# SyncE fetches 102 token columns in place of 96 and ScalarE 62 in place of 52, with other pacing tables

## The chip, the cores and the metric

One core of a Trainium2 chip runs the whole kernel; the other cores are idle. The metric is the device time of one execution in microseconds (us), lower being better. The time before is the median of three runs.

## What is computed

The reference looks up rows of embedding tables for 16384 samples, averages them, joins them and passes them through a small network. The part that matters here is the first lookup: 32 token rows of 300 floats (1200 bytes) per sample, out of a table of 50000 rows, averaged over the 32.

```python
tok = word_emb[token_idx].mean(axis=1)      # (16384, 32) indices, rows of 300 floats
e1 = emb_mh1[mh1_idx].mean(axis=1)          # 20 indices per sample; e2, e3 likewise
o1 = emb_oh1[oh1_idx]                       # 1 index per sample; o2, o3, o4 likewise
emb = concatenate([tok, e1, e2, e3, o1, o2, o3, o4], axis=1)
wide = ...                                  # sums of one more column of the same small tables
h = relu(emb @ W1 + b1); h = relu(h @ W2 + b2); h = relu(h @ W3 + b3)   # 748 -> 1024 -> 512 -> 256
y = sigmoid(h @ Wd + bd + wide)
```

## The kernel before

**Tiles and steps.** The batch is cut into 128 tiles of 128 samples. One Python loop (`for step in range(n_steps)`) writes out the program of all engines: a tile has 11 steps, and 27 more steps (`WAKE`) let the last tiles finish, 1435 in all. Each engine runs its own instructions in the order in which this loop wrote them, and waits on semaphores where one needs another's result.

**What a step does.** VectorE compares indices with a counter and writes one-hot rows (`hot`, the group `hot<-own,sc`). ScalarE scales a half of them (`hot<-hot`), which is the "one-hot scaling" of the change. TensorE multiplies one-hots into counts (`pc<-hot`), ScalarE copies the counts out (`cnt<-pc`), TensorE multiplies counts with the small tables (`pg<-terms,cnt`), and VectorE sums that into the features (`g<-pg`). Beside this TensorE runs the network's layers (`ph<-x,w_sb`, `ph<-odd,w_sb`, `ph<-even,w_sb`), whose results ScalarE copies out (`odd<-ph`, `even<-ph`).

**Token rows.** For one sample tile and one of the 32 token positions, 128 rows have to be fetched. The text calls this a *column*. There are 128 x 32 = 4096 columns, and three ways to fetch one:

- GpSimd (POOL) issues one indirect DMA for the whole column (`gather`, L260, `tok_rows<-in_word_emb_dram,it`). Two columns make a group, 16 groups a tile; there are six buffers of one group each (`TOK_BUFS`), and a group is added three groups after it was asked for (`TOK_LAG`).
- SyncE (SP) issues 128 plain DMAs of one row each (`row`, L244, `fetched<-in_word_emb_dram`). It first reads the 128 row addresses into registers, 32 at a time (`load`, L275, a `TENSOR_LOAD`), so a column is four times one load and 32 rows. The indices themselves come by one DMA per column (`load_column`, L233, `columns<-in_idx_dram`), and VectorE turns them into byte offsets (`column_offsets`, `columns<-columns`). SP may fetch token position 31 of a tile, and has two buffers (`FETCH_BUFS`).
- ScalarE (ACT) does the same for token position 30 (`fetched_scalar<-in_word_emb_dram`), with 16 addresses per load. Its rows stand in its queue before and after the one-hot scaling of each step (`scalar_rows(step, SCALAR_BEFORE)`, then `one_hots`, then `scalar_rows(step, SCALAR_AFTER)`).

VectorE adds each column to the tile's sum in PSUM (`own<-own,tok_rows`, `own<-own,fetched`), and the last add of a tile writes the features (`g<-own,...`). These adds stand in one queue with the one-hots of the following steps.

**Who fetches what** is settled when the program is written, by `RowFetches`. It lays fetches of a fixed length (`steps`) end to end, and gives each one the next tile that is not needed before that fetch ends plus `FETCH_MARGIN`, three steps. A column that neither SP nor ACT takes goes to POOL. `wanted_at(t)` is the step in which tile t's sum is due: `16 / 1.4196 = 11.27` steps from tile to tile. Before, `FETCH_STEPS` is 14.5 steps for a column on SP: the first starts at step 31.16 and serves tile 5, the last starts at step 1408.66 and serves tile 127, 96 columns in all. ACT puts out five rows a step (25.6 steps a column), 52 columns. POOL keeps 4096 - 96 - 52 = 3948.

`prepare` has the column's indices loaded four steps ahead of the start of its fetch, and the offsets computed one step ahead (`COLUMN_AHEAD`, `COLUMN_LAG`). SP's queue also holds the index loads of each pair of tiles (`it`, `ix`) and the stores of results (`out_dram<-x`), all L233.

Of the kernel before, what the change touches and what calls it, by code (L numbers as in the profile page):

```python
# [22 lines left out]
N_TOK, TOK_D = 32, 300  # L23
# [5 lines left out]
TOK_BUFS = 6  # L29
HOT_BUFS = 2  # L30
FETCH_FROM = 4
FETCH_STEPS = 14.5
FETCH_MARGIN = 3.0
FETCH_BUFS = 2
COLUMN_AHEAD = 4
# [1 line left out]
LOADS = 32  # L37
LANES = 8
ROW_SEMAPHORES = 8
SCALAR_FROM = 8  # L40
SCALAR_BEFORE, SCALAR_AFTER = 3, 2
SCALAR_RATE = SCALAR_BEFORE + SCALAR_AFTER
SCALAR_MARGIN = 5.0
SCALAR_LOADS = 16
# [332 lines left out]
def kernel(  # L377
# [679 lines left out]
    tiles = B // P  # L1057
# [13 lines left out]
    def summed_at(t):  # L1071

        n = n_groups * (t + 1) + TOK_LAG
        return n / FRONT_PACE if n < front else FRONT_STEPS + (n - front) / pace
# [2 lines left out]

        return summed_at(t) - 1.0

    by_sync = RowFetches(N_TOK - 1, False, summed_at(FETCH_FROM) - FETCH_STEPS - FETCH_MARGIN, FETCH_STEPS, tiles, LOADS)  # L1080
    scalar_steps = P / SCALAR_RATE
    by_scalar = RowFetches(
        N_TOK - 2, True, int(summed_at(SCALAR_FROM) - scalar_steps - SCALAR_MARGIN), scalar_steps, tiles - 2, SCALAR_LOADS
    )
    sync_rows = Paced_rows(by_sync, FETCH_STEPS)

# [162 lines left out]
```

## Time and profile before

| | |
|---|---|
| time before, median of 3 runs | 4987.18 us (4986.96 to 4992.43) |
| profiled execution: time, span | 4988.4 us, 4986.6 us |
| granted TensorE clock, mean | 0.991 |
| busy: TensorE, VectorE, ScalarE, GpSimd | 4794.8, 3642.8, 2728.2, 3739.3 us |
| token columns by POOL, SP, ACT | 3948, 96, 52 |
| rows issued one by one by SP, ACT | 12288, 6656 |

The span runs from the first to the last instruction. In the lines below, PE is TensorE, PEld its weight loads, DVE VectorE, ACT ScalarE, POOL GpSimd, SP SyncE. A "q" behind a name (SPq, ACTq) is the engine's sequencer, which issues DMAs and loads registers; this is not counted as busy, so SP has no busy time at all. "x3948" counts instructions. In a group, "busy, mean ns of one" is followed by the idle time of the engine just ahead of these instructions and what ended it; "issue" means that nothing in the profile ended it. TensorE's busy time is modelled and includes pipelined waiting.

### The profile page before, as it was taken

What the parts mean: (1) busy time and instruction counts of PE and PEld (TensorE: products, weight loads), DVE (VectorE), ACT (ScalarE), POOL (GpSimd) and SP (SyncE); (2) the same over time, 40 slices, a digit from 0 to 9 for tenths busy, and PEclk for the clock granted to TensorE, in tenths of its full rate; (3) what the DMA queues carried; (4) which work ended last, traced back from release to release, by engine and by line L of the source; (5) the groups of instructions that cost most, each with busy time, mean ns of one, the idle gap of its engine ahead of it and who ended that gap; (6) DMA issues with size and microseconds to landing.
All of it is one profiled execution on the core that took longest, in us unless ns stands there. A gap on an engine that the chain in (4) does not pass through costs nothing.

```text
span 4986.6 us, 110478 instructions
## 1 busy us (share of the span) xinstructions
PE 4794.8 (96%) x36356; PEld 3712.3 (74%) x36356; DVE 3642.8 (73%) x6908; ACT 2728.2 (55%) x3658; POOL 3739.3 (75%) x3955
## 2 busy tenths in 40 slices
PE   6699999999999999999999999999999999999999
PEld 4577777777777777777777777767767888888898
DVE  5777777777777777777777777777777777777763
ACT  5455555555555555555555555555555555555552
POOL 7777777777777777777777777777777777777765
PEclk9899999999999999999999999999999999999999
DMA  7444444444444444444444444444444444444443
GB/s 204 127 130 130 130 131 129 131 130 130 131 131 131 130 130 130 131 131 130 130 131 130 131 131 130 130 131 129 131 130 130 130 131 130 131 131 130 131 120 95
DMA packets 305354, 653.28 MB, mean 131 GB/s; under 512 B 157083, under 2 KB 176667, under 8 KB 304775
## 3 DMA queue, kind: packets, MB, share of 16 engines
q0 software_dynamic: 189504, 606.67, 44.7%
q1 hardware_dynamic: 94471, 31.50, 2.9%
q10 hardware_dynamic: 20800, 8.04, 0.8%
q8 instruction: 284, 4.65, 0.4%
q14 instruction: 295, 2.42, 0.2%
HBM read 645.67 MB, written 0.07 MB: 129 GB/s over the span
## 4 chain that ended last, share of the span: by engine, by line
PE 46%; POOL 16%; DMA 15%; DVE 12%; issue 8%; ACT 1%; ACTq 1%; SPq 1%; DVEq 0%; POOLq 0%
PE ph L113 24%; PE pg L113 16%; POOL tok_rows L260 16%; DMA tok_rows<-in_word_emb_dram,it 15%; PE pc L113 6%; DVE own L113 5%; DVE hot L113 4%; DVE g L113 1%; ACTq L244 1%; SPq L244 1%; ACTq L275 0%; ACT cnt L113 0%; DVE x L113 0%; DVE columns L113 0%; ACT hot L113 0%
## 5 line engine op out<-in xcount | busy, mean ns | idle before, releaser
L260 POOL DMA_INDIRECT tok_rows<-in_word_emb_dram,it x3948 | 3738.4, 947 | 1215.6 <-issue 931.5
L113 DVE TENSOR_TENSOR own<-own,tok_rows 128x300 f32<-128x300 f32 x3601 | 1714.5, 476 | 822.0 <-DMA tok_rows<-in_word_emb_dram,it 746.8
L113 ACT ACTIVATE hot<-hot 64x768 bf16<-64x768 bf16 (+1 forms) x1408 | 1155.3, 821 | 1698.2 <-DVE hot L113 1514.8
L113 PE MATMUL pg<-terms,cnt 128*128 128x195 bf16 x17664 | 1721.6, 249 | 31.0 <-DVE g L113 30.7
L113 PEld LDWEIGHTS pg<-terms,cnt 128*128 128x128 fp8e3 x17664 | 1523.8, 98 | 83.7 <-DVE g L113 39.1
L113 PE MATMUL ph<-x,w_sb 128*128 128x384 f32 (+5 forms) x4932 | 1472.1, 436 | 16.5 <-ACT odd L113 11.3
L113 DVE TENSOR_TENSOR hot<-own,sc 128x1656 bf16<-128x1656 bf16 (+1 forms) x1408 | 1386.6, 985 | 86.0 <-PE pc L113 80.4
L113 ACT ACTIVATE cnt<-pc 128x828 uint16<-128x828 f32 (+1 forms) x1408 | 1186.3, 843 | 257.0 <-PE pc L113 170.8
L113 PEld LDWEIGHTS ph<-x,w_sb 128*128 128x128 f32 (+1 forms) x4932 | 829.8, 191 | 306.5 <-ACT odd L113 20.9
L113 PE MATMUL ph<-odd,w_sb 128*128 128x384 f32 (+2 forms) x3328 | 983.2, 434 | 7.7 <-ACT odd L113 7.3
L113 PEld LDWEIGHTS pc<-hot 128*128 128x128 bf16 x8192 | 589.5, 98 | 494.8 <-issue 217.6
L113 PE MATMUL pc<-hot 128*128 128x138 bf16 x8192 | 733.2, 225 | 92.0 <-ACT hot L113 58.7
L113 PEld LDWEIGHTS ph<-odd,w_sb 128*128 128x128 f32 x3328 | 558.7, 191 | 204.7 <-ACT odd L113 15.8
L113 DVE TENSOR_REDUCE g<-pg 128x130 f32<-128x390 f32 (+1 forms) x512 | 259.7, 507 | 216.0 <-PE pg L113 213.1
L113 ACT ACTIVATE odd<-ph,b_sb 128x384 f32<-128x384 f32 (+2 forms) x515 | 270.0, 524 | 134.4 <-PE ph L113 68.8
L113 PE MATMUL ph<-even,w_sb 128*128 128x384 f32 (+2 forms) x832 | 250.0, 436 | 3.3 <-ACT even L113 2.9
L113 PEld LDWEIGHTS ph<-even,w_sb 128*128 128x128 f32 x832 | 142.3, 191 | 56.8 <-ACT even L113 4.1
L113 DVE TENSOR_TENSOR x<-pc,scale 128x768 f32<-128x768 f32 x127 | 120.9, 952 | 74.8 <-PE pc L113 74.0
L113 ACT ACTIVATE even<-ph,b_sb 128x384 f32<-128x384 f32 (+2 forms) x208 | 108.7, 523 | 88.4 <-PE ph L113 65.8
L113 PE MATMUL pc<-ident,g 128*128 128x128 f32 x762 | 106.5, 276 | 11.7 <-ACT cnt L113 7.5
L113 PEld LDWEIGHTS pc<-ident,g 128*128 128x128 f32 x762 | 82.9, 142 | 15.8 <-ACT cnt L113 11.7
L113 DVE COPY sc<-pc 128x512 bf16<-128x512 bf16 x64 | 44.0, 687 | 55.1 <-PE pc L113 55.0
(54 smaller groups left out, 673.0 us busy)
## 6 DMA issues: line engine op xcount, KB each, us to landing
fetched<-in_word_emb_dram SPq DMA_DIRECT2D x12288, 1.2 KB
fetched_scalar<-in_word_emb_dram ACTq DMA_DIRECT2D x6656, 1.2 KB
tok_rows<-in_word_emb_dram,it POOLq DMA_INDIRECT x3948
ix<-in_idx_dram SPq DMA_DIRECT2D x64, 64.0 KB
w_sb<-in_W_dram SPq DMA_DIRECT2D x6, 512.0 KB
it<-in_idx_dram SPq DMA_DIRECT2D x64, 32.0 KB
w_sb<-in_W_dram SPq DMA_DIRECT2D x1, 2048.0 KB
odd<-in_mh_dram SPq DMA_DIRECT2D x3, 682.5 KB
```

The costliest lines, as they stand in the source:

```text
L113: lambda: call(*args, **operands), self.name, self.name, aps + list(named.values()), outs
L244: return queue.add_instruction(mybir.InstDMACopy(name=self.nc.get_next_instruction_name(), engine=queue.engine, mode="Copy", ins=whole(sou ...
L260: return self.nc.gpsimd.indirect_dma_start(out=out, out_offset=None, in_=table, in_offset=bass.IndirectOffsetOnAxis(ap=index, axis=0),)
```

## The change

```diff
-FETCH_STEPS = 14.5
+FETCH_STEPS = 13.5
...
-SCALAR_BEFORE, SCALAR_AFTER = 3, 2
+SCALAR_BEFORE, SCALAR_AFTER = 4, 2
 SCALAR_RATE = SCALAR_BEFORE + SCALAR_AFTER
...
-    by_sync = RowFetches(N_TOK - 1, False, summed_at(FETCH_FROM) - FETCH_STEPS - FETCH_MARGIN, FETCH_STEPS, tiles, LOADS)
+    by_sync = RowFetches(N_TOK - 1, False, summed_at(FETCH_FROM) - FETCH_STEPS - FETCH_MARGIN, FETCH_STEPS, tiles - 1, LOADS)
```

A column on SP is given 13.5 steps in place of 14.5. The planner then places 102 columns: the first starts at step 32.16 and serves tile 5 as before; the last two start at steps 1382.16 and 1395.66 and serve tiles 124 and 126. Tile 127 is no longer open to SP (`tiles - 1`). ACT puts out six rows a step, so a column has 21.33 steps, and it gets 62 columns. POOL keeps 4096 - 102 - 62 = 3932. TensorE's instructions and their order stay the same.

ScalarE's queue about a sixth into the program, where `hot_76` and `hot_77` are the two one-hot buffers, `cnt` the counts and L244 a token row, before:

```order
1216 L113 ACTIVATE hot_76<-hot_76 64x6x128
1217 L244 DMA fetched_scalar_83<-in_word_emb_dram 1x1200 x2
1218 L113 ACTIVATE cnt_78<-pc_95 128x138x6
1219 L244 DMA fetched_scalar_83<-in_word_emb_dram 1x1200 x3
1220 L113 ACTIVATE hot_77<-hot_77 64x6x128
1221 L275 TENSOR_LOAD columns
1222 L244 DMA fetched_scalar_82<-in_word_emb_dram 1x1200 x2
```

and after:

```order
1217 L113 ACTIVATE cnt_78<-pc_95 128x138x6
1218 L244 DMA fetched_scalar_83<-in_word_emb_dram 1x1200 x4
1219 L113 ACTIVATE hot_77<-hot_77 64x6x128
1220 L275 TENSOR_LOAD columns
1221 L244 DMA fetched_scalar_83<-in_word_emb_dram 1x1200 x2
1222 L113 ACTIVATE cnt_78<-pc_94 128x138x6
```

One more row stands between a copy of the counts and the next one-hot scaling.

VectorE's queue at the end of tile 9's token sum, where `tok_rows` are columns of POOL, `fetched_80` a column of SP, and `hot` the one-hots of the next steps, before:

```order
382 L113 TENSOR_TENSOR hot_77<-own,sc_74 128x1656
383 L113 TENSOR_TENSOR own<-own,tok_rows_64 128x300
384 L113 TENSOR_TENSOR g_84<-own,tok_rows_64 128x300
385 L113 COPY sc_75<-pc_94 128x2x128x2
386 L113 TENSOR_TENSOR hot_76<-own,sc_74 128x1656
```

and after:

```order
382 L113 TENSOR_TENSOR hot_77<-own,sc_74 128x1656
383 L113 TENSOR_TENSOR own<-own,fetched_80 128x300
384 L113 TENSOR_TENSOR g_84<-own,tok_rows_64 128x300
385 L113 COPY sc_75<-pc_94 128x2x128x2
386 L113 TENSOR_TENSOR hot_76<-own,sc_74 128x1656
```

Tile 9 is one of the tiles whose last column comes from SP now and came from POOL before; the one-hots of the next step stand behind its add.

SP's queue at the end of the program, where `fetched_80` and `fetched_81` are its two buffers and `out_dram` the stores of results, before:

```order
1266 L244 DMA fetched_81<-in_word_emb_dram 1x1200 x32
1267 L275 TENSOR_LOAD columns
1268 L244 DMA fetched_81<-in_word_emb_dram 1x1200 x13
1269 L233 DMA out_dram<-x 1x128
1270 L244 DMA fetched_81<-in_word_emb_dram 1x1200 x19
1271 L233 DMA out_dram<-x 1x128 x3
```

and after:

```order
1326 L244 DMA fetched_81<-in_word_emb_dram 1x1200 x13
1327 L275 TENSOR_LOAD columns
1328 L244 DMA fetched_81<-in_word_emb_dram 1x1200 x32
1329 L275 TENSOR_LOAD columns
1330 L244 DMA fetched_81<-in_word_emb_dram 1x1200 x32
1331 L233 DMA out_dram<-x 1x128 x5
```

The last row of SP's last column has moved ahead of two more stores, since that column serves tile 126 in place of 127.

## Prediction

> **What bounds the kernel now.** I began with the page: the costliest groups and the list of DMA issues.
>
> ```profile
> PE 4794.8 (96%) x36356; PEld 3712.3 (74%) x36356; DVE 3642.8 (73%) x6908; ACT 2728.2 (55%) x3658; POOL 3739.3 (75%) x3955
> L260 POOL DMA_INDIRECT tok_rows<-in_word_emb_dram,it x3948 | 3738.4, 947 | 1215.6 <-issue 931.5
> L113 DVE TENSOR_TENSOR own<-own,tok_rows 128x300 f32<-128x300 f32 x3601 | 1714.5, 476 | 822.0 <-DMA tok_rows<-in_word_emb_dram,it 746.8
> ...
> fetched<-in_word_emb_dram SPq DMA_DIRECT2D x12288, 1.2 KB
> fetched_scalar<-in_word_emb_dram ACTq DMA_DIRECT2D x6656, 1.2 KB
> ```
>
> TensorE looks fullest, but its busy time is modelled. POOL shows 75%, yet its idle time is mostly "issue", that is, nothing held it. The timeline of POOL and the stretches say what that means:
>
> ```profile
> 2009.62 0.94 POOL L260 DMA_INDIRECT tok_rows<-in_word_emb_dram,it  x1 [0.30 <-issue]
> 2010.87 0.94 POOL L260 DMA_INDIRECT tok_rows<-in_word_emb_dram,it  x1 [0.30 <-issue]
> ...
> 500.00:1000.00 500.00, 491.04 (x3608) 361.25 (x3606) 372.84 (x708) 278.30 (x361) 378.02 (x401) 0.99 0.49 130
> 4000.00:4500.00 500.00, 495.17 (x4055) 439.25 (x4054) 375.33 (x707) 286.20 (x396) 377.99 (x401) 1.00 0.49 131
> ```
>
> A gather starts every 1.25 us (0.94 and 0.30 of issue), and early as well as late 401 of them fill 500 us (the fifth engine column): 401 x 1.25 = 501. POOL has no gap, and VectorE waits 746.8 us for its columns. POOL sets the pace, and TensorE is close behind.
>
> The page shows no busy time for SP at all, so I asked for its queue: the timeline of SP, then its register loads over the whole span and in three stretches (first and last start stand behind the durations).
>
> ```profile
> 2013.42 5.69 SPq L244 DMA_DIRECT2D fetched<-in_word_emb_dram  x18
> 2019.15 0.56 SPq L233 DMA_DIRECT2D columns<-in_idx_dram  x1
> 2019.76 45.20 SPq L244 DMA_DIRECT2D fetched<-in_word_emb_dram  x123
> ...
> L275 SPq TENSOR_LOAD <-columns x384: 2025/2127/2391, 142.9 to 4905.2; - x192
> L275 SPq TENSOR_LOAD <-columns x25: 2042/2127/2178, 1835.7 to 2129.9; - x25
> L275 SPq TENSOR_LOAD <-columns x28: 2026/2127/2192, 844.4 to 1176.4; - x28
> L275 SPq TENSOR_LOAD <-columns x41: 2030/2128/2289, 4218.2 to 4713.9; - x41
> ...
> L113 DVE TENSOR_SCALAR columns<-columns x296: 203/218/477, 142.4 to 4870.7; 1x128 int32<-1x128 int32 x148
> ```
>
> Four loads make a column. Over the span a column comes every 4 x (4905.2 - 142.9) / 383 = 49.74 us; in the three stretches every 49.03 (24 intervals), 49.19 (27) and 49.57 (40). The plan gives it 14.5 steps. A step lasts (4870.7 - 142.4) / 1377 = 3.434 us, since the offsets of SP's first and last column are computed in steps 30 and 1407. So the plan's 14.5 steps are 49.8 us, and SP uses nearly all of them: it is the second engine at its limit, and the page hides it.
>
> **The change, part by part.**
>
> *POOL loses 16 gathers*: 16 x 1.25 = 20 us less. This is all the gain there is: a span of 4967, if nothing else binds.
>
> *SP gets 13.5 steps a column*: 13.5 x 3.434 = 46.4 us, and 46.2 with POOL's relief. What does SP need? From below, built up from rows: the stretch of 123 rows above holds four loads, so a row takes (45.20 - 4 x 2.127) / 123 = 0.298 us. The rest of its queue is in this view of L233:
>
> ```profile
> L233 SPq DMA_DIRECT2D columns<-in_idx_dram x96: 534/554/606, 100.7 to 4852.5; - x96
> L233 SPq DMA_DIRECT2D it<-in_idx_dram x64: 402/414/3305, 1.0 to 4709.5; - x64
> L233 SPq DMA_DIRECT2D ix<-in_idx_dram x64: 589/612/1623, 1.5 to 4709.9; - x64
> L233 SPq DMA_DIRECT2D out_dram<-x x52: 217/785/835, 316.2 to 4981.2; - x52
> ```
>
> 128 x 0.298 + 4 x 2.127 + 0.55 = 47.2; it, ix and out add 64 x (0.414 + 0.612) + 52 x 0.785 = 106 us, 1.1 a column: 48.3 us. From above: 49.6, the slowest stretch. I take 48.9: the fastest stretch (49.03), as nothing there can be less than SP's work by much, less 0.1 because the 106 us are spread over 102 columns. SP is then short of 2.5 us in each column and falls behind the plan for good. The slack of a single column (3 to 14 steps between its planned end and its tile's due step) is used up within about ten columns. From there on VectorE stands at `own<-own,fetched`, the next one-hots stand behind it in its queue, and ScalarE, TensorE and (when the six buffers are full) POOL behind these. The kernel becomes as slow as SP's queue.
>
> How long is that queue? The first column's load starts one step later than before, 142.9 + 3.4 = 146.3. The tile of the last column but one (124) is due 4.5 steps after its planned end, so this one is late and the last is not: tile 126 is due 27 steps after that column's start, and the last column needs 14.2. So 101 columns count: 146.3 + 101 x 48.9 = 5085. What follows tile 124's sum was in the trace of before:
>
> ```profile
> 4846.28 0.47 DVE L113 TENSOR_TENSOR g<-own,fetched_scalar 128x300 f32<-128x300 f32 x1
> 4881.91 29.36 SPq L244 DMA_DIRECT2D fetched<-in_word_emb_dram  x79
> ...
> 4954.79 0.95 POOL L260 DMA_INDIRECT tok_rows<-in_word_emb_dram,it  x1 [0.31 <-DVE own L113]
> 4959.97 0.47 DVE L113 TENSOR_TENSOR g<-own,tok_rows 128x300 f32<-128x300 f32 x1
> ```
>
> From 4846.3 to the end of the span, 4986.6, are 140 us, with as many gathers as after, but for one. I add 3 us for the landing of the last rows (an estimate; a gather took 3.49 us in the chain). POOL can then be three groups ahead, six gathers or 7.5 us, but TensorE is at 96% and can hardly follow, so I take nothing off. The sum is 5085 + 3 + 140 = 5228 of span. Against the span before that is +241: 102 columns short of 2.5 us, less some 14 of slack. The profiled execution took 4988.4, 1.2 above the median, and its span 0.6 below it; so 5229 on the median's scale.
>
> *ScalarE* issues 10 columns more: 1280 rows and 80 loads. What stands around them, in its timeline and the waits:
>
> ```profile
> 1998.37 3.49 DMA tok_rows<-in_word_emb_dram,it
> 2006.96 0.81 ACTq L244 DMA_DIRECT2D fetched_scalar<-in_word_emb_dram  x3
> 2007.82 0.84 ACT L113 ACTIVATE hot<-hot 64x768 bf16<-64x768 bf16 x1 [0.29 <-DVE hot L113]
> ...
> L275 ACTq TENSOR_LOAD <-columns x416: 1178/1294/1532, 255.1 to 4816.2; - x139
> ACT hot L113 <- DVE hot L113: 1514.8, 947, 5.7
> DVE own L113 <- DMA fetched<-in_word_emb_dram: 11.2, 3, 6.7
> ```
>
> (The first line is the chain's gather, used above.) A row is 0.27 us, 3 in 0.81. The queue grows by 1280 x 0.27 + 80 x 1.29 = 449 us over the run. In 947 of 1408 steps ScalarE came early to the scaling and waited for VectorE, 1.6 us on average, so the fourth row lies in that wait. In the other 461 it can lengthen the step by up to 0.27, 124 us in all at most; but each step has 2.5 / 13.5 = 0.19 us to spare once SP sets the pace, which covers most of it. I cost it at 0 and keep 0 to 40 for the range. If SP did not bind, this cover would be gone.
>
> *The rest*: VectorE computes offsets for 16 more columns, two instructions each of 0.22, 7 us spread over a VectorE that is idle a quarter of the time: nothing. Its adds are as many as before. Rows of SP and ACT may get in each other's way a little more; the 0.298 holds that as it was, and I leave it to the range.
>
> **The rivals.**
>
> *SP keeps up, and the gain comes through.* For that a row would have to take (46.4 - 8.5 - 0.55 - 1.1) / 128 = 0.283 us, or waits must hide in the 49. Against it: no stretch shows less than 49.03 a column. Then 4967, faster by 0.4%; the point of decision is 46.4 us a column. The Trainium skill's "DMA: Bandwidth & Descriptors", section "Issuing engines are not separate DMA queues", says that starting DMAs from several engines only saves the issue time on the sequencer, and that this is usually small next to the DMA itself. By it SP would have room, and this rival would hold. The trace does not agree here: 128 issues at 0.298 us fill SP's sequencer.
>
> *SP is slower than 46.4, but less so: part of the 49 is waiting.* What speaks for it is the view of SP's waits:
>
> ```profile
> SPq L275 <- DVE own L113: 220.3, 73, 43.4
> SPq L275 <- DVE hot L113: 27.7, 13, 3.8
> SPq L275 <- DVE g L113: 13.6, 4, 6.5
> ```
>
> Without the first wait (43.4, ahead of the first column) that is 218 us. If all of it were real, a column would need 49.74 - 218 / 96 = 47.5, and the span would be 146 + 101 x 47.5 + 143 = 5086. But the view finds a release up to the end of an instruction, and each of these loads lasts 2.13 us by itself, 90 x 2.13 = 192: most of the 218 is the loads.
>
> *ScalarE becomes a second brake.* If each step lengthened by 0.27 on top of SP's pace (the row ahead of the scaling, with PE waiting behind it), 461 to 1408 steps would add 124 to 380 us: some 5350 to 5600. The waits above speak against it.
>
> *No change*: SP would need just about 46.5 us. Nothing points there.
>
> **How the numbers follow.** SP-bound at 48.3 to 49.6 a column: 0.85, span 5167 to 5299 by 101 x -0.6 and 101 x 0.7. SP part waiting: 0.06, near 5086. ScalarE a second brake: 0.04. SP keeps up: 0.03. No change: 0.02. The range of 5175 to 5285 leaves out the other cases and the outer edges of the first, where the build-up (48.3) and the slowest stretch (49.6, with late waits) are least likely. Within 0.2% (10 us) counts as no change.
>
> **What would show it.** In the changed kernel's trace: SP's loads at an even 48.9 us a column up to about 5130, in place of 49.74 with waits; POOL's idle time ended by `DVE own`, with fewer than 401 gathers in 500 us (about 380); a wait of `DVE own` for `fetched` of 200 us or more in all, where there were three of 11.2 us in all; the chain of waits running through SP's rows; ScalarE's waits for `hot` longer, not shorter. I am wrong if SP's loads come every 46.4 us, or if POOL still starts a gather every 1.25 us throughout.

## The result and the profile after

The changed kernel takes 5280.68 us (median of 4 runs, 5274.67 to 5283.33), the kernel before 4987.07 on the same chip: a ratio of 1.0585 [1.0566, 1.0603], 5.9% slower. The forecast was 5229 with a range of 5175 to 5285. The profiled execution took 5282.48 us, its span 5280.7.

The page of the changed kernel: busy time, the chain of waits by engine and by line, the costliest group, and the list of DMA issues.

```profile
PE 4875.9 (92%) x36356; PEld 3763.6 (71%) x36356; DVE 3643.8 (69%) x6940; ACT 2732.5 (52%) x3658; POOL 3726.0 (71%) x3939
PE 41%; SPq 32%; DVE 8%; issue 7%; DMA 5%; POOL 2%; ACT 2%; ACTq 2%; DVEq 0%
SPq L244 25%; PE ph L113 22%; PE pg L113 14%; SPq L275 6%; PE pc L113 5%; DVE hot L113 3%; DVE own L113 3%; DMA columns<-in_idx_dram 3%; POOL tok_rows L260 2%; DMA tok_rows<-in_word_emb_dram,it 2%; ACTq L244 1%; ACT hot L113 1%; SPq L233 1%; DVE g L113 1%; ACT cnt L113 1%
L260 POOL DMA_INDIRECT tok_rows<-in_word_emb_dram,it x3932 | 3725.1, 947 | 1520.5 <-issue 905.4
...
fetched<-in_word_emb_dram SPq DMA_DIRECT2D x13056, 1.2 KB
fetched_scalar<-in_word_emb_dram ACTq DMA_DIRECT2D x7936, 1.2 KB
```

Every engine does what it did before, in nearly as much busy time (TensorE 1.7% more), and has lost share: no engine with busy time has become the bound. POOL's group costs 13 us less, and its idle time is 305 us more (1215.6 before). What has entered the chain is SP: its queue holds 32% of it, the 128-row columns (L244) first and their register loads (L275) second. Before, it held 1%, and POOL 16%:

```profile
PE 46%; POOL 16%; DMA 15%; DVE 12%; issue 8%; ACT 1%; ACTq 1%; SPq 1%; DVEq 0%; POOLq 0%
```

SP's register loads over the span (count, duration ns min/median/max, first and last start), and two stretches of 500 us (busy time and count of PE, PEld, DVE, ACT and POOL, granted clock, DMA share, GB/s):

```profile
L275 SPq TENSOR_LOAD <-columns x408: 2026/2127/2372, 145.0 to 5149.4; - x136
500.00:1000.00 500.00, 466.82 (x3324) 341.49 (x3322) 351.28 (x669) 260.97 (x339) 352.64 (x373) 0.97 0.46 122
2500.00:3000.00 500.00, 472.53 (x3381) 346.37 (x3380) 353.84 (x675) 263.04 (x342) 357.28 (x379) 0.98 0.47 124
```

A column of SP comes every 4 x (5149.4 - 145.0) / 407 = 49.18 us. The plan wanted 13.5 steps of 3.434 us, 46.4. SP got faster by 0.56 us a column (49.74 before), and no more. POOL gets 373 to 379 gathers into 500 us, where 401 went before.

Where the lateness arrives is in the view of waits (us in total, times, longest), the first two lines of before, the others of the changed kernel:

```profile
DVE own L113 <- DMA tok_rows<-in_word_emb_dram,it: 769.8, 757, 4.3
POOL tok_rows L260 <- DVE own L113: 166.0, 510, 3.3
...
POOL tok_rows L260 <- DVE own L113: 436.4, 650, 13.3
ACT hot L113 <- DVE own L113: 340.9, 262, 3.2
DVE columns L113 <- DMA columns<-in_idx_dram: 291.9, 71, 8.5
DVE own L113 <- DMA fetched<-in_word_emb_dram: 182.6, 20, 15.1
DVE own L113 <- DMA tok_rows<-in_word_emb_dram,it: 121.2, 105, 5.1
```

VectorE used to wait for POOL's columns, 769.8 us in all. It now waits 121.2 for those, and 474.5 us for what comes out of SP's queue: the rows themselves (182.6) and, which the forecast did not foresee, the indices of the column four steps ahead (291.9), whose load stands in the same queue between SP's rows. POOL then waits for VectorE: 436.4 us, 166.0 before.

One such hold in the timelines of VectorE, SP and POOL:

```profile
4957.60 1.01 DVE L113 TENSOR_TENSOR hot<-own,sc 128x1656 bf16<-128x1656 bf16 x1
4972.35 0.48 DVE L113 TENSOR_TENSOR own<-own,fetched 128x300 f32<-128x300 f32 x1 [13.73 <-DMA fetched<-in_word_emb_dram]
4972.86 0.47 DVE L113 TENSOR_TENSOR g<-own,fetched_scalar 128x300 f32<-128x300 f32 x1
...
L275 SPq TENSOR_LOAD <-columns x1: 2114/2114/2114, 4966.5 to 4966.5; - x1
...
4961.24 0.95 POOL L260 DMA_INDIRECT tok_rows<-in_word_emb_dram,it  x1 [0.30 <-issue]
4974.91 0.94 POOL L260 DMA_INDIRECT tok_rows<-in_word_emb_dram,it  x1 [12.73 <-DVE own L113]
```

VectorE stands 13.73 us at the add of a column of SP (tile 120). POOL puts out one more gather at 4961.24 with 0.30 us of issue before it, then its buffers are full and it stands 12.73 us, until VectorE has gone on. It looks like the chain of the forecast: SP late, VectorE at its add, POOL behind. Which of SP's rows the add waits for is another matter; the section on the prediction comes back to it. The 13.73 us are the time of four steps.

### The profile page after: what moved, and what is told of

Its sections match the earlier page's. It is cut to its first block, busy times and chain, and to the rows that moved or that the text cites. A ratio compares the mean times of both kernels' runs of the same rounds, so it can differ in the third digit from the quotient of the medians.

```text
span 5280.7 us, 112655 instructions
## 1 busy us (share of the span) xinstructions
PE 4875.9 (92%) x36356; PEld 3763.6 (71%) x36356; DVE 3643.8 (69%) x6940; ACT 2732.5 (52%) x3658; POOL 3726.0 (71%) x3939
## 4 chain that ended last, share of the span: by engine, by line
PE 41%; SPq 32%; DVE 8%; issue 7%; DMA 5%; POOL 2%; ACT 2%; ACTq 2%; DVEq 0%
SPq L244 25%; PE ph L113 22%; PE pg L113 14%; SPq L275 6%; PE pc L113 5%; DVE hot L113 3%; DVE own L113 3%; DMA columns<-in_idx_dram 3%; POOL tok_rows L260 2%; DMA tok_rows<-in_word_emb_dram,it 2%; ACTq L244 1%; ACT hot L113 1%; SPq L233 1%; DVE g L113 1%; ACT cnt L113 1%
## 5 line engine op out<-in xcount | busy, mean ns | idle before, releaser
L113 PE MATMUL pg<-terms,cnt 128*128 128x195 bf16 x17664 | 1751.6, 251 | 38.1 <-DVE g L113 38.0
L113 PEld LDWEIGHTS pg<-terms,cnt 128*128 128x128 fp8e3 x17664 | 1549.8, 99 | 93.0 <-DVE g L113 42.5
L113 PE MATMUL ph<-x,w_sb 128*128 128x384 f32 (+5 forms) x4932 | 1495.2, 441 | 28.0 <-ACT odd L113 23.5
L113 PEld LDWEIGHTS ph<-x,w_sb 128*128 128x128 f32 (+1 forms) x4932 | 842.1, 193 | 325.2 <-ACT odd L113 30.2
L113 PE MATMUL ph<-odd,w_sb 128*128 128x384 f32 (+2 forms) x3328 | 998.6, 439 | 13.6 <-ACT odd L113 13.1
L113 DVE TENSOR_SCALAR columns<-columns 1x128 int32<-1x128 int32 x328 | 80.5, 246 | 299.6 <-DMA columns<-in_idx_dram 291.9
L113 DVE TENSOR_TENSOR own<-own,fetched 128x300 f32<-128x300 f32 x102 | 48.2, 472 | 183.4 <-DMA fetched<-in_word_emb_dram 182.6
```

Of the source, the lines that this page charges most:

```text
L113: lambda: call(*args, **operands), self.name, self.name, aps + list(named.values()), outs
```

## The experiments

Theory A is the forecast's: SP needs about 49 us a column, the plan gives 46.4, and SP's queue sets the end. Against it stood: ScalarE's fourth row is the brake; the wait for the indices is a loss of its own; the threshold is all or nothing. Each ratio is against the kernel before on the same chip; an edit is shown against the changed kernel unless the text says otherwise.

**Each half of the change alone.** First only ScalarE's half:

```diff
-FETCH_STEPS = 13.5
+FETCH_STEPS = 14.5
...
-by_sync = RowFetches(..., tiles - 1, LOADS)
+by_sync = RowFetches(..., tiles, LOADS)
```

> ScalarE's part alone: six rows a step, 62 columns on ScalarE, SP back at 96 columns and 14.5 steps; POOL keeps 3938 gathers. Theory A (SP's queue sets the end of the changed kernel): SP again has 49.8 us for a column that needs about 49.2, so POOL sets the pace and the ten gathers fewer come through: 10 x 1.25 = 12.5 us, 4975 us (4968 to 4983). Rival B (the fourth row ahead of the one-hot scaling lengthens the steps): slower than before, 5030 us or more.

Then only SP's half:

```diff
-SCALAR_BEFORE, SCALAR_AFTER = 4, 2
+SCALAR_BEFORE, SCALAR_AFTER = 3, 2
```

> SP's part alone: 102 columns at 13.5 steps, ScalarE back at three and two rows and 52 columns. Theory A: SP's loads come every 49.2 us a column as in the changed kernel, and the time is the same, 5281 us (5265 to 5290). Rival B: with the fourth row gone the time falls by what that row cost, to 5200 us or less.

ScalarE's half alone: 4981.86 us, ratio 0.9990 [0.9981, 1.0000]. SP's half alone: 5278.90 us, ratio 1.0585 [1.0567, 1.0602], the whole loss. SP's loads and the waits, of ScalarE's half and then of SP's:

```profile
L275 SPq TENSOR_LOAD <-columns x384: 2025/2127/2362, 143.0 to 4903.2; - x192
DVE own L113 <- DMA fetched<-in_word_emb_dram: 11.7, 3, 6.3
```

```profile
L275 SPq TENSOR_LOAD <-columns x408: 2027/2126/2378, 145.0 to 5151.5; - x136
DVE columns L113 <- DMA columns<-in_idx_dram: 304.6, 69, 9.2
DVE own L113 <- DMA fetched<-in_word_emb_dram: 191.3, 20, 15.1
```

With 52 columns on ScalarE SP still comes every 4 x (5151.5 - 145.0) / 407 = 49.2 us, so ScalarE's extra rows neither slow SP's queue nor the step. That rival is out. ScalarE's half gained 5 us of the 12.5 that ten gathers cost (10 x 1.25). Part of the difference shows late in the program, in two stretches of 200 us of ScalarE's half:

```profile
4000.00:4200.00 200.00, 197.69 (x1603) 174.64 (x1601) 145.74 (x275) 111.57 (x156) 149.25 (x158) 1.00 0.48 129
4600.00:4800.00 200.00, 193.75 (x1736) 177.45 (x1736) 144.03 (x272) 112.17 (x167) 147.60 (x156) 1.00 0.48 128
```

POOL puts out 158 and 156 gathers where 160 fit (161 and 158 before), and TensorE is busy 97 to 99%, as before: the gathers taken from POOL no longer make it faster there, and TensorE is probably the next limit. This reading was not tested by itself.

**Indices earlier.** Is the index wait (291.9 us) a loss of its own, or only where SP's lateness shows first?

```diff
-COLUMN_AHEAD = 4
+COLUMN_AHEAD = 8
```

> The changed kernel with the indices of a column asked for eight steps ahead of its fetch in place of four. VectorE's new wait for these indices (columns from in_idx, 292 us in the changed kernel's trace) should fall under 60 us. Theory A: that wait is only the form in which SP's lateness reaches VectorE; it comes back as a wait for the fetched rows, SP's pace stays at 49.2 us a column, and the time at 5265 to 5285 us. Rival C (the wait for indices, not the number of rows in SP's queue, is what costs): 5281 - 200 or more, under 5100 us.

5274.29 us, ratio 1.0574 [1.0557, 1.0592], 6 us better than the change. The waits and SP's loads:

```profile
DVE columns L113 <- DMA columns<-in_idx_dram: 29.7, 11, 6.2
DVE own L113 <- DMA fetched<-in_word_emb_dram: 381.7, 27, 28.6
L275 SPq TENSOR_LOAD <-columns x408: 2023/2127/2397, 144.7 to 5141.0; - x136
```

262 us of one wait went, and 199 us came in another. SP's column stays at 4 x (5141.0 - 144.7) / 407 = 49.1. A wait that is removed while the queue behind it stays too long is only moved.

**Half a step back.** If SP's need is about 49.2 us, 14.0 steps (48.1 us) should be short by 1.1 us a column and not by 2.8.

```diff
-FETCH_STEPS = 13.5
+FETCH_STEPS = 14.0
```

> The changed kernel with 14.0 steps a column on SP in place of 13.5: 99 columns. Theory A: 14.0 steps are 48.0 us, short of 49.2 by 1.2 us a column; SP's queue ends about 150 us earlier, and the time is about 5105 us (5080 to 5125), still slower than before. Rival D (slower only because the plan is pressed past a threshold of slack, in all or nothing): 4970 or 5280 us.

5093.88 us, ratio 1.0213 [1.0196, 1.0230], with 99 columns on SP.

```profile
L275 SPq TENSOR_LOAD <-columns x396: 2023/2128/2384, 142.9 to 5001.3; - x198
DVE columns L113 <- DMA columns<-in_idx_dram: 162.7, 49, 7.2
DVE own L113 <- DMA fetched<-in_word_emb_dram: 106.1, 11, 14.0
```

Again 4 x (5001.3 - 142.9) / 395 = 49.2 us a column, whatever the plan says; the loss follows the shortfall times the columns and is not all or nothing. As a rough sum, with the plan's slack and POOL's relief left aside, 98 x 1.1 = 108 us, measured 107; with 13.5 steps 101 x 2.8 = 283, measured 294.

**A dearer queue under the old plan.** The sharpest test leaves all columns where they were before and makes only SP's queue dearer: eight loads of 16 addresses in place of four of 32 (against the kernel before).

```diff
-LOADS = 32
+LOADS = 16
```

> The kernel of e7_loads16 a third time: the kernel before with SP reading its addresses 16 at a time, eight loads a column in place of four; the same 96 columns and 3948 gathers. Where the kernel before takes its 4987 us, theory A: a column on SP grows from 49.0 to about 50.7 us, over its 49.8, and the kernel takes 5050 us (5030 to 5080), with VectorE waiting for SP's rows; rival B (only the moved columns or ScalarE matter): 4987 us. Where the kernel before takes over 7000 us, a step lasts about 4.9 us and SP's column has 71 us: no difference over 0.3%.

5053.61 us against 4987.70, ratio 1.0134 [1.0117, 1.0151]. POOL has all its 3948 gathers, ScalarE all its rows.

```profile
L275 SPq TENSOR_LOAD <-columns x768: 1135/1232/1492, 142.9 to 4977.7; - x192
DVE columns L113 <- DMA columns<-in_idx_dram: 202.3, 58, 7.7
DVE own L113 <- DMA fetched<-in_word_emb_dram: 36.6, 9, 12.3
POOL tok_rows L260 <- DVE own L113: 260.8, 637, 9.5
```

Eight loads of 1.232 us are 1.35 us more than four of 2.127. A column comes every 8 x (4977.7 - 142.9) / 767 = 50.43 us where the plan gives 49.8, and the same waits appear as in the changed kernel, smaller. So SP's queue sets the time in both, and with 32 addresses a load the kernel before stood just under that line.

**Two kernels on a chip where this program is slower.** The same test was first made on another chip, twice, and with it the opposite one: the changed kernel with a cheaper queue, 112 rows of a column singly and the last 16 partitions by one DMA of table rows 0 to 15. That kernel leaves out the fetch of those 16 rows.

```diff
+if not by_scalar and p >= P - 16:
+    if p == P - 1:
+        rest = dict(out=tile_rows[P - 16 : P, :], in_=word[0:16, :])
+        program.record(lambda: queue.dma_start(**rest), "SP", lane, [], [rest["out"]], batch=batch)
...
```

> The kernel before with SP reading its addresses 16 at a time in place of 32: eight loads a column in place of four. In the changed kernel's trace a load of 16 on ScalarE took 1.26 us, a load of 32 on SP 2.13. Theory A: a column on SP grows from 49.0 to 49.0 + 8 x 1.30 - 4 x 2.17 = 50.7 us, over its 49.8; the same 96 columns and 3948 gathers become slower, 5050 us (5030 to 5080), with VectorE waiting for SP's rows. Rival B (only the moved columns or ScalarE matter): no change, 4987 us.

> The kernel of e7_loads16 again, on a chip where the kernel before takes its 4987 us: the kernel before with SP reading addresses 16 at a time, eight loads a column. Theory A: a column on SP grows from 49.0 to about 50.7 us, over its 49.8, and the kernel takes 5050 us (5030 to 5080). Rival B (only the moved columns or ScalarE matter): 4987 us.

> The changed kernel with 112 of SP's 128 rows fetched one by one; the last 16 partitions of each of SP's columns get rows 0 to 15 of the table by one DMA, so those token rows are other rows than the indices name. All else stands, ScalarE's part too. Theory A: SP's column falls from 49.2 to 49.2 - 16 x 0.30 + 0.4 = 44.8 us, under the 46.3 that the plan gives it; SP is off the path, POOL and TensorE set the pace again, and all of the loss goes: 4965 to 4985 us. Rival B (ScalarE's or VectorE's added work brakes as well): part of the loss stays, over 5020 us.

> The kernel of e6_rows112 again, on a chip where the kernel before takes its 4987 us: 112 of SP's 128 rows one by one, the last 16 partitions by one DMA of table rows 0 to 15 (other rows than the indices name). Theory A: SP's column falls from 49.2 to 44.8 us, under the 46.3 of the plan, and all of the loss goes: 4965 to 4985 us. Rival B (ScalarE's or VectorE's added work brakes as well): over 5020 us. If the chip is again one where the kernel before takes over 7000 us, the run says nothing on this.

> The kernel of e6_rows112 a third time (112 of SP's 128 rows one by one; the last 16 partitions get table rows 0 to 15 by one DMA). Where the kernel before takes its 4987 us, theory A: SP's column falls under the 46.3 us of the plan and all of the loss goes: 4965 to 4985 us; rival B: over 5020 us. Where the kernel before takes over 7000 us, steps last 4.9 us, SP has 66 us a column, and theory A expects no difference that matters, as in the two runs before: within 1%.

On that chip the kernel before itself takes 7136 to 7142 us. The eight loads gave 1.0004 [0.9984, 1.0024] and 1.0012 [0.9990, 1.0034]; the 112 rows 1.0035 [1.0018, 1.0053] and 1.0027 [1.0007, 1.0046], and a third time, on a further chip where the kernel before takes 7242 us, 1.0044 [1.0027, 1.0061]. SP's loads and a group of TensorE in the second run of eight loads:

```profile
L275 SPq TENSOR_LOAD <-columns x768: 3/1224/1488, 192.1 to 7070.7; - x192
L113 PE MATMUL pg<-terms,cnt 128*128 128x195 bf16 x17664 | 2049.5, 266 | 823.2 <-issue 603.4 <-DVE g L113 217.6 <-DVE own L113 0.4
```

SP's column comes every 8 x (7070.7 - 192.1) / 767 = 71.7 us there, some 21 us more than its queue needs, because each step is some 4.9 us long; a queue that is dearer by 1.35 us a column is then hidden, as theory A has it (1.0004 and 1.0012 against 1.0134). The 112 rows, though, had no chance to show a gain there: what a cheaper queue would give where SP sets the pace stays open.

**Two more plans on the same chip.** The changed kernel with 14.25 steps a column (97 columns on SP), and the kernel before with seven rows a step on ScalarE (73 columns):

```diff
-FETCH_STEPS = 13.5
+FETCH_STEPS = 14.25
```

> The changed kernel with 14.25 steps a column on SP, 97 columns. Theory A: 14.25 steps are 48.9 us, 0.3 us short of 49.2 a column; the slack of the plan holds most of that: 4992 us (4978 to 5010). If the loss set in at 14.5 already, it would lie halfway between 4982 and 5094, 5038 us.

```diff
-SCALAR_BEFORE, SCALAR_AFTER = 3, 2
+SCALAR_BEFORE, SCALAR_AFTER = 4, 3
```

> SP as in the kernel before (96 columns, 14.5 steps), ScalarE with four rows ahead of the scaling and three behind: 73 columns, POOL 3927. By POOL alone 21 x 1.25 = 26 us less than 4987: 4961. ScalarE's part alone gave 5 of 12.5 us, so I expect 4976 us (4965 to 4988). Rival B: the seventh row lengthens the steps, over 4995 us.

They came to 1.0074 [1.0056, 1.0092] and 1.0103 [1.0085, 1.0122], on the chip with the long step, where SP has room. Neither tells about the chips on which a step lasts 3.434 us. On the slower chips all five kernels in which ScalarE issues six or seven rows a step (these two and the three with 112 rows) are 0.3 to 1.0% slower, with intervals clear of no change, and the two with five rows are not; whether ScalarE's rows cause it there was not tested. Where between 14.0 and 14.5 steps the line lies, and whether ScalarE can carry more than 62 columns, stays open.

The best kernel of all these is ScalarE's half alone, 4981.86 us, and its interval reaches up to no change.

## Why the prediction was right, and where its sizes were off

**SP as the hidden second bound: right.** Two views carried it, the loads of SP over the span and in stretches, on a page that gives SP no busy time. SP's column took 49.2 us under plans of 46.4 and 48.1, with ScalarE at 62 or 52 columns, so it is what the queue needs in this program, with little waiting in it (0.23 us a column, see below): the rival in which part of the 49 was waiting (47.5 a column, 5086) is out, and so is the one in which SP keeps up (4967). The second of these is what the Trainium skill would give ("DMA: Bandwidth & Descriptors", "Issuing engines are not separate DMA queues": the issue time is usually small next to the DMA). The measurement differs and decides: 128 issues, four loads and the rest fill 49.2 us, and dearer loads alone cost 1.3%.

**The size of a column: 48.9 forecast, 49.2 measured.** Over 98 columns the 0.30 us are 29 us; the first load came 1.3 us earlier than forecast. Most of the 0.30 is a wait within SP's own queue (its rows that wait for VectorE's adds, before and after):

```profile
SPq L244 <- DVE own L113: 7.1, 4, 2.5
SPq L244 <- DVE own L113: 23.3, 16, 2.3
```

23.3 us over 102 columns are 0.23 us a column, so the queue's own work is close to the 48.9 of the forecast. The sum had this wait at nothing; where it comes from is told below, with the two adds of buffer `fetched_80`.

**The end: the last late tile was 120, not 124.** This is the step that failed, and it is worth 24 us. The forecast had column 100 (tile 124) as the last one that holds VectorE. But tiles 122 to 124 came 42 to 45 us apart, and from tile 120's last add to tile 124's it took as long as before. The adds of tile 120 and 124 before and of tile 124 after (tile 120's is shown above), and the two stretches between them, before and after:

```profile
4682.20 0.47 DVE L113 TENSOR_TENSOR g<-own,fetched_scalar 128x300 f32<-128x300 f32 x1
4846.28 0.47 DVE L113 TENSOR_TENSOR g<-own,fetched_scalar 128x300 f32<-128x300 f32 x1
...
5136.92 0.47 DVE L113 TENSOR_TENSOR g<-own,fetched_scalar 128x300 f32<-128x300 f32 x1
...
4684.00:4848.00 164.00, 157.46 (x1534) 149.40 (x1532) 112.41 (x209) 92.70 (x146) 118.42 (x126) 1.00 0.46 124
4975.00:5140.00 165.00, 157.93 (x1504) 149.00 (x1503) 113.61 (x211) 92.83 (x148) 114.83 (x122) 0.98 0.44 119
```

Both took 164.1 us, with TensorE busy 96% of the time; TensorE probably sets that pace, and VectorE waited for no row of SP any more. The last hold is the one shown above: tile 120, released when SP began column 98 at 4966.5. From that load to the end of the span are 314.2 us; the forecast's own terms had 3 x 48.9 + 3 + 140 = 289.7 there. So the sum is 28 us (pace and first load) + 24.5 us (the end) = 52.5, the span of 5280.7 against the 5228 of the forecast.

Tile 120 is served by column 96, whose rows SP had put out before it began column 97, so its add should have been free about a column earlier. The reason is in VectorE's queue, with the semaphores of SP's eight lanes of rows (column k is on lane k modulo 8):

```
6609 L113 TENSOR_TENSOR own<-own,fetched_80 128x300 [waits sem_SProws2,sem_DVE]
...
6716 L113 TENSOR_TENSOR own<-own,fetched_80 128x300 [waits sem_SProws2,sem_DVE]
```

The first add is column 96's, and it waits for lane 2, that of column 98, which is written into the same buffer (`fetched_80`). With 13.5 steps a column and two buffers, the program writes the first rows of column k+2 ahead of column k's add where the plan leaves a tile more than about 13 steps of slack. The queues hold 14 such adds now and held 3 before. A column that looked most comfortable in the plan thus waits for SP to begin the next but one. SP stands there too: it puts out nine rows of column 98, and the tenth, into the same buffer, has to wait until the add has read it. In the changed kernel the ninth row starts at 4970.9 and the tenth at 4972.9, where 0.3 us lie between two rows otherwise:

```profile
L244 SPq DMA_DIRECT2D fetched<-in_word_emb_dram x2: 212/228/243, 4970.9 to 4972.9; - x2
```

At the 14 adds this comes to nearly all of the 23.3 us above, so the same order of the program accounts for most of the error in the pace and for the hold at tile 120. That a kernel without it would have come to the forecast's 5228 was not shown: a third buffer was not tried. The measured time lies 4 us inside the upper end of the range, which was set for a slower pace and not for such an order; that the range holds it is in part luck.

The order has a second consequence. At such an add the first 4 to 13 rows of column k+2 already stand in the buffer in place of column k's, so the sum takes token rows of another tile: 113 of SP's 13056 rows in the changed kernel, and 16 of 12288 before. Both kernels have this fault, and a plan with two buffers has to exclude it.

**How the lateness reaches the others: right in kind, nearly all of it by other roads.** POOL stands behind `DVE own` with 373 to 379 gathers in 500 us (about 380 forecast), and the chain runs through SP's rows. The wait for `fetched` is 182.6 us in 20 places (200 or more forecast). But 174.1 of it stand at the 14 adds that wait for the next column but one. Only 8.5 us, in six places of 0.4 to 2.5, are an add's wait for its own column, which is what the forecast meant; the three waits of before (11.2 us) were at the three adds of this kind as well. The larger new wait, 291.9 us for a column's indices, was not in the forecast, though the load L233 was quoted in it as part of SP's queue: what stands in a saturated queue is late as well, small things too. The earlier indices showed that it costs nothing of its own but some 6 us; with them the waits for an add's own column came to 110.6 us of the 381.7.

**ScalarE at 0: right.** Its rows cost nothing with SP as the bound (5280.68 against 5278.90) nor without (4981.86, 5 us below before). The sign named for it was wrong, though: its waits for `DVE hot` went from 1514.8 us to

```profile
ACT hot L113 <- DVE hot L113: 1409.5, 729, 15.4
```

fewer and less in sum, with a longest of 15.4 where 5.7 stood. What grew is the wait for `DVE own` (130.0 to 340.9). The two halves alone, ScalarE's first, divide this:

```profile
ACT hot L113 <- DVE hot L113: 1393.5, 872, 5.5
ACT hot L113 <- DVE own L113: 250.9, 200, 3.0
...
ACT hot L113 <- DVE hot L113: 1512.0, 819, 15.0
ACT hot L113 <- DVE own L113: 211.3, 187, 1.9
```

With the fourth row alone 121 us move from the one wait to the other and the sum stays what it was before (1644 us). With SP's half alone the sum grows by 79. So more of the growth in `DVE own` goes with the fourth row than with SP's lateness; why the wait moves was not looked into.

**POOL's 20 us: not realised, as forecast.** POOL has 16 gathers fewer and 305 us more of idle time.

## What to carry to other kernels

An engine that only issues DMAs can be the next limit while the page shows no busy time for it: take the pitch of a regular instruction in its queue and set it against the time that the plan gives. When several producers share a job and each is near its limit, moving work from the bound to the next one pays only up to that one's own rate; past it the loss is the shortfall per item times the number of items, here 2.8 us on a hundred columns against 20 us to be gained. And the end of such a sum needs its own look: which item is the last late one depends on who paces the tail and on whether an instruction has been written behind its buffer's next fill; where it has, it may also read the wrong data.

## What the runs showed of the hardware beyond that

A register load of SP takes 2.127 us for 32 values and 1.232 us for 16. Two sizes on a line make an estimate of 0.056 us a value and 0.34 us fixed, so fewer and larger loads are cheaper in a saturated queue.

TensorE's granted clock, a mean of 0.991 before, fell to 0.968 with the stalls. Two stretches of 50 us of the changed kernel (columns as above), the first with the hold at tile 120, the second without one:

```profile
4950.00:5000.00 50.00, 38.91 (x290) 34.25 (x289) 26.38 (x47) 18.53 (x26) 26.60 (x29) 0.86 0.35 93
5150.00:5200.00 50.00, 48.94 (x480) 47.93 (x479) 24.22 (x51) 13.55 (x30) 36.99 (x39) 1.00 0.44 122
```

0.86 with 39 us of TensorE's work in 50, 1.00 with 49: a wait that empties TensorE goes with a lower clock around it; what that adds to the loss was not measured by itself.

On two chips the same program takes 7136 to 7242 us instead of 4987. The traces there show gathers of 947 ns as ever, a clock of 0.88, and TensorE standing where the profile shows nothing that it waited for: 603.4 us of "issue" ahead of the `pg` group quoted above, 0.2 us before on the first chip. VectorE and ScalarE wait there for something that the profile calls `remote` (in the same run 1000.7 us ahead of VectorE's one-hots and 1475.7 ahead of ScalarE's copies of the counts), which no trace of the faster chips has. The cause was not found.
